# A four-layer image network on one NeuronCore: the parts of the last layer reordered into eighteen steps over six images, the adjusting in two halves

## The chip, the cores and the metric

The kernel runs on one NeuronCore of one Trainium2 chip. The metric is the device time of one execution in microseconds (us). The engines are named as in the profile: PE is TensorE (matrix multiplies, with PEld for its weight loads), DVE is VectorE, ACT is ScalarE, POOL is GpSimd, and SP is the engine whose queue starts the transfers. Each engine runs its own instructions in the order in which the program issues them; what one engine needs from another it waits for by semaphores.

## The reference, cut to what matters

The input is 32 images of 128 channels and 32 x 32 pixels, in float32. Four layers are applied, each as `x = x + layer(group_norm(x))`. The first is a 3 x 3 convolution, the second a state-space layer over the pixels, the third makes per-row and per-column maps with two more state-space scans, the fourth simulates a circuit of four qubits for each pixel. The change concerns the place where the third layer's maps are applied and the whole fourth layer:

```python
# end of layer 2: the maps of rows and columns are multiplied out, mixed, and scale the image
result_h = sigmoid(a_h) * x_y
result_w = sigmoid(a_w) * x_x
out1 = conv1x1(concatenate([result_h, result_w], axis=1), adjust_w)
return x * out1
...
# layer 3, on group_norm(x)
xq = xf @ pre_w.T + pre_b            # four angles for each pixel
z = simulate(xq, q_weights)          # sixteen amplitudes, squared and summed
out = z @ post_w.T + post_b
```

`group_norm` takes mean and variance over groups of four channels of one image.

## The kernel before

`images` and `attention` compute the first three layers up to the maps of rows and columns (`self.maps`), which stay in SBUF; the images themselves lie in DRAM as `self.x2`. The method `tail` then does the rest, image by image, with an image as a tile of 128 channels by 1024 pixels. It works through a software pipeline: a *turn* `j` issues each part once, for image `j - behind`, and `order` lists the parts with their distance `behind`. `manual_schedule` keeps the order of issue as written, so `order` is also the order of the instructions on each engine. A load of image `j` (`begin`) opens each turn.

What each part issues, and on which engine:

| part | instructions | lines |
|---|---|---|
| `begin` | SP: load of `xt`, 512 KB | L1407 |
| `outer` | POOL: products `rh`, `rw`; ACT: normalized image `xn` from `xt` | L1412, L1413, L1415 |
| `adjust` | PE: `adj` from `rh` and `rw`, two halves of 512 pixels | L1424, L1425 |
| `adjusted` | DVE: `xn` times `adj`, by halves; POOL: `xt` plus `xn` | L1430, L1431 |
| `sums` | DVE: statistics of the new `xt`, twice, and their union `gn_ag` | L1436, L1438 |
| `mean` | PE: means over the group of four channels | L1442 |
| `spread` | DVE: copy, difference, square (`gn_mv`, `gn_dv`) | L1446, L1447, L1448 |
| `variance` | PE: variance over the group | L1454 |
| `root` | DVE: add a constant; POOL: power -0.5 | L1457, L1458 |
| `normal` | DVE: `gn_mv`; ACT: x4, the normalized image | L1462, L1466 |
| `angles` | PE: `q` from x4, 16 rows for each half | L1471 |
| `rounded` | DVE: whole turns `kk` of the angles, two instructions | L1477, L1478 |
| `sines` | DVE: the rest `rr`; ACT: sine in place | L1482, L1485 |
| `states` | PE: `psi`, the amplitudes | L1490 |
| `squares` | ACT: `sq` | L1497 |
| `outputs` | PE: `outs`, two halves | L1503 |
| `end` | DVE: `xt` plus `outs`, two halves; SP: store of `xt`, 512 KB | L1510, L1513 |

The matrix products are in float32, so the profile shows two matmul instructions for each product of the program. Each product goes to a bank of PSUM of its own: two each for `adj` and `outs`, one each for `mean`, `variance`, `q` and `psi`, eight in all. `xt` has six buffers, all other tiles of an image three.

Of the kernel before, what the change touches and what calls it, by code (L numbers as in the profile page):

```python
# [12 lines left out]
F32 = mybir.dt.float32  # L13
BF16 = mybir.dt.bfloat16
AF = mybir.ActivationFunctionType
ALU = mybir.AluOpType
# [3 lines left out]
P = 128  # L20
S = 32
HW = S * S
# [532 lines left out]
class Steps:  # L555
# [11 lines left out]
    def run(self, ways, plan):  # L567

        k = self.k
        steps = [(w, h, n) for w in ways for h in range(2) for n in range(DS)]  # L570
        self.steps = steps
        for i in range(3):
            self.load(i)
        for i in range(3):
            self.decay(i)
        self.spread(0)
        self.input(0)
        for i in range(len(steps) + 2):
            self.evict()
            self.decay(i + 3)  # L580
            k.flush(False, vector=False)
            self.spread(i + 1)
            self.catch_up()
            self.scan(i)
            k.flush(False)
            self.input(i + 1)
            if self.has(i):
                plan.slot(i, self.load_of(i))
            self.scale(i + 4)
            self.weigh(i)  # L590
            self.add(i - 2)
            self.load(i + 3)
        self.evict()
        k.flush()
# [148 lines left out]
class Kernel:  # L743
# [630 lines left out]
    def tail(self):  # L1374
        tc, nc, d = self.tc, self.nc, self.d
        with ExitStack() as ctx:
            par = ctx.enter_context(tc.tile_pool(name="par3", bufs=1))
            img = ctx.enter_context(tc.tile_pool(name="img3", bufs=3))
            psl = ctx.enter_context(tc.tile_pool(name="psl3", bufs=3, space=PSUM))
            adj = par.tile([P, 2, P], F32, name="adj")  # L1380
# [14 lines left out]
            halves = [(32 * c, slice(c * 512, (c + 1) * 512)) for c in range(2)]  # L1395
# [7 lines left out]

            def begin(im, i):
                im.i = i
                im.xt = img.tile([P, HW], F32, tag="xt", name="xt", bufs=6)
                nc.sync.dma_start(im.xt, self.x2[i])  # L1407

            def outer(im):
# [7 lines left out]
                    scale=self.means[:, im.i, 2 * L + 1 : 2 * L + 2],  # L1417
                )

            def adjust(im):  # L1420
                im.adj = []
                for _, cs in halves:
                    ps = bank("adj", 2)
                    nc.tensor.matmul(ps, adj[:, 0], im.rh[:, cs], start=True, stop=False)  # L1424
                    nc.tensor.matmul(ps, adj[:, 1], im.rw[:, cs], start=False, stop=True)  # L1425
                    im.adj.append(ps)

            def adjusted(im):
                for ps, (_, cs) in zip(im.adj, halves):
                    nc.vector.tensor_tensor(im.xn[:, cs], im.xn[:, cs], ps, ALU.mult)  # L1430
                nc.gpsimd.tensor_tensor(im.xt, im.xt, im.xn, ALU.add)  # L1431

            def sums(im):
                st = tile_([P, 2, 6], "gn_st")
# [73 lines left out]
            def end(im):  # L1508
# [5 lines left out]


            order = [
                (sums, 3), (angles, 4), (mean, 3), (rounded, 4), (spread, 3), (variance, 3), (sines, 4),
                (root, 3), (adjust, 2), (states, 4), (adjusted, 2), (normal, 3), (squares, 4),
                (outputs, 4), (outer, 1), (end, 4),
            ]  # L1520
            with tc.manual_schedule():
                for j in range(self.n + 4):
                    if j < self.n:
                        begin(images[j], j)
                    for part, behind in order:
                        if 0 <= j - behind < self.n:
                            part(images[j - behind])
# [20 lines left out]
```

## Time and profile before

| quantity | value |
|---|---|
| median of 3 runs | 15073.83 us |
| lowest and highest of them | 15066.03 and 15084.82 us |
| profiled execution, its own time | 15093.06 us |
| its span | 15091.3 us |
| first instruction of `tail` on POOL (L1412) | 14599.22 us |
| time from there to the end of the span | 492.1 us |
| busy in the whole span: PE, DVE, ACT, POOL | 87%, 89%, 81%, 84% |
| busy in the 60 us from 14820 to 14880: PE, DVE, ACT, POOL | 41.03, 27.52, 13.97, 26.51 us |
| mean granted TensorE clock in these 60 us | 0.78 |

Lines of the profile read as follows. A group of instructions is given as line of the kernel, engine, operation, tile written, tiles read, shapes and count. On the timeline a row begins with the start and the duration in us; in brackets stand the idle time of the engine ahead of it and what ended it. In the list of waits, `A <- B: total, times, longest` says how long the first engine stood still ahead of that line until the second one's line was done. The three runs give the time that counts; the profile gives places and durations, from one execution that was 19.2 us longer than their median.

### The profile page before, as it was taken

What the parts mean: (1) busy time and instruction counts of PE and PEld (TensorE: products, weight loads), DVE (VectorE), ACT (ScalarE), POOL (GpSimd) and SP (SyncE); (2) the same over time, 40 slices, a digit from 0 to 9 for tenths busy, and PEclk for the clock granted to TensorE, in tenths of its full rate; (3) what the DMA queues carried; (4) which work ended last, traced back from release to release, by engine and by line L of the source; (5) the groups of instructions that cost most, each with busy time, mean ns of one, the idle gap of its engine ahead of it and who ended that gap; (6) DMA issues with size and microseconds to landing.
All of it is one profiled execution on the core that took longest, in us unless ns stands there. A gap on an engine that the chain in (4) does not pass through costs nothing. (4 is left out here: it accounts for less than half of the span.)

```text
span 15091.3 us, 197699 instructions
## 1 busy us (share of the span) xinstructions
PE 13174.8 (87%) x70318; PEld 8507.7 (56%) x70318; DVE 13401.1 (89%) x8776; ACT 12256.2 (81%) x21181; POOL 12747.8 (84%) x6529
## 2 busy tenths in 40 slices
PE   7888888888888888988888888888888888888876
PEld 4555555555555555555555555555555555555532
DVE  7999989999989999898999999999999999999774
ACT  6888888888888888888888888888888888888642
POOL 6888888888888888888888888888888888888764
PEclk8999999999999999999999999999999999999877
DMA  3444444444444444444444444444444444444431
GB/s 118 159 155 155 156 153 154 156 159 156 155 153 153 158 155 159 154 154 154 153 157 159 154 157 153 155 152 158 157 157 154 155 153 154 157 159 157 144 107 68
DMA packets 633895, 2277.61 MB, mean 151 GB/s; under 512 B 77481, under 2 KB 81145, under 8 KB 632777
## 3 DMA queue, kind: packets, MB, share of 16 engines
q1 hardware_dynamic: 630600, 2263.06, 43.8%
q8 instruction: 554, 9.08, 0.2%
q14 instruction: 437, 3.57, 0.1%
q10 hardware_dynamic: 2304, 1.90, 0.0%
HBM read 2221.35 MB, written 43.33 MB: 150 GB/s over the span
## 5 line engine op out<-in xcount | busy, mean ns | idle before, releaser
L686 POOL TENSOR_TENSOR hh<-hh,cc 128x1024 f32<-128x1024 f32 x4160 | 9771.8, 2366 | 1752.5 <-DVE hh L677 1086.5
L677 DVE TENSOR_TENSOR_SCAN hh<-da,bu 128x1024 f32<-128x1024 f32 x4160 | 9415.4, 2280 | 618.6 <-PE bu L647 234.9
L722 PEld LDWEIGHTS y<-cbig,hh 128*128 128x128 f32 x33280 | 4065.2, 150 | 1793.5 <-issue 1285.2
L722 PE MATMUL y<-cbig,hh 128*128 128x128 f32 x33280 | 4762.6, 290 | 181.8 <-POOL hh L686 181.4
L633 ACT ACTIVATE da<-dt,m_na 128x1024 f32<-128x1024 f32 x4096 | 4607.2, 1144 | 352.8 <-DVE hh L677 344.9
L669 DVE TENSOR_TENSOR bu<-du,bu 128x1024 f32<-128x1024 f32 x2752 | 3336.8, 1213 | 680.5 <-PE bu L653 679.6
L662 ACT ACTIVATE but<-dut,bt 128x128 f32<-128x128 f32 x11264 | 3433.6, 392 | 0.0
L653 PE MATMUL bu<-parts,sel 48*128 48x512 bf16 x5504 | 1761.5, 402 | 638.6 <-DVE hh L677 630.0
L280 PE MATMUL mm<-hpad,m_wc 128*128 128x512 f32 x4096 | 2063.6, 627 | 104.1 <-ACT relu L386 68.6
L647 PE MATMUL bu<-cbig,but 128*128 128x128 f32 x11264 | 1606.7, 290 | 378.1 <-DVE hh L677 331.6
L647 PEld LDWEIGHTS bu<-cbig,but 128*128 128x128 f32 x11264 | 1388.4, 151 | 445.2 <-issue 287.8
L280 PEld LDWEIGHTS mm<-hpad,m_wc 128*128 128x128 f32 x4096 | 710.1, 193 | 908.6 <-issue 753.5
L653 PEld LDWEIGHTS <-sel 48*128 48x128 bf16 x5504 | 322.6, 95 | 1149.9 <-DVE hh L677 687.2
L402 POOL TENSOR_TENSOR w<-w,du 128x1024 f32<-128x1024 f32 x260 | 613.8, 2361 | 38.3 <-ACT w L395 38.3
L299 PE MATMUL mm<-uc,m_xw 128*128 128x512 f32 x1024 | 602.9, 720 | 31.0 <-ACT sz L762 22.6
L701 PEld LDWEIGHTS y<-m_skip,uc 128*128 128x128 f32 x4096 | 554.4, 212 | 132.8 <-issue 79.8
L762 ACT ACT_TABLE_LOAD x483 | 619.7, 1283 | 8.5
L768 ACT ACT_TABLE_LOAD x483 | 619.7, 1283 | 8.5
L439 ACT COPY dut<-mm 128x512 f32<-128x512 f32 x512 | 294.9, 576 | 407.0 <-PE mm L434 406.9
L406 POOL TENSOR_TENSOR dt<-dt,w 128x1024 f32<-128x1024 f32 x260 | 615.3, 2366 | 0.2
L411 POOL TENSOR_TENSOR du<-dt,uc 128x1024 f32<-128x1024 f32 x260 | 614.3, 2363 | 0.2
L406 POOL TENSOR_TENSOR dt<-dt,relu 128x1024 f32<-128x1024 f32 x260 | 613.9, 2361 | 0.0
(219 smaller groups left out, 10394.3 us busy)
## 6 DMA issues: line engine op xcount, KB each, us to landing
cc<-rows SPq DMA_DIRECT2D x4160, 512.0 KB, 3.8
xt<-in_x SPq DMA_DIRECT2D x32, 512.0 KB, 5.9
x<-xt SPq DMA_DIRECT2D x32, 512.0 KB, 3.7
xt<-x SPq DMA_DIRECT2D x32, 512.0 KB, 4.0
out<-xt SPq DMA_DIRECT2D x32, 512.0 KB, 2.9
rows<-dbl SPq DMA_DIRECT2D x130, 64.0 KB, 4.3
stats<-st SPq DMA_DIRECT2D x32, 36.0 KB, 1.5
means<-stats SPq DMA_DIRECT2D x1, 1152.0 KB
```

Of the source, the lines that this page charges most:

```text
L280: nc.tensor.matmul(self.view(ps), m.wc[:, v, j, h * P : (h + 1) * P], self.taps(j, c), start=(j == 0), stop=(j == 3),)
L406: nc.gpsimd.tensor_tensor(self.dt[h], self.dt[h], t[name], op)
L633: k.nc.scalar.activation(t, w.dt[h], AF.Exp, scale=w.m.na[:, h, n : n + 1])
L647: k.nc.tensor.matmul(t[:, b * P : (b + 1) * P], but[:, b], k.ident, start=True, stop=True, is_transpose=True,)
L653: k.nc.tensor.matmul(t[:, cs], k.sel[:, n], w.parts[:, cs], start=True, stop=True)
L662: k.nc.scalar.activation(t[:, b], w.dut[h][:, b], AF.Copy, scale=w.bt[:, b, n : n + 1])
L669: k.nc.vector.tensor_tensor(t, w.du[h], t, ALU.mult)
L677: k.nc.vector.tensor_tensor_scan(way(t), way(self.da.pop(i)), way(self.bu.pop(i)), 0.0, ALU.mult, ALU.add)
L686: k.nc.gpsimd.tensor_tensor(t, t, self.cc.pop(i), ALU.mult)
L722: k.nc.tensor.matmul(self.y[g][: w.bl, b], t[:, at], k.ident, start=False, stop=(n == DS - 1 and b == w.per - 1), is_transpose=True,)
L762: self.nc.scalar.activation(*args, AF.Silu, **kw)
L768: self.nc.scalar.preload_act_table_set("natural_log_exp_and_others")
```

## The change

The order has eighteen steps instead of sixteen, since `adjust` and `adjusted` are each split into the two halves of 512 pixels. The distances are spread over six images instead of four: `adjust` and `adjusted` stay at 2 turns behind the load, the statistics (`sums` to `normal`) move from 3 to 4, the circuit from `angles` to `squares` from 4 to 5, and `outputs` and `end` from 4 to 6. The last turn is therefore `n + 5` instead of `n + 3`. `outer` moves from near the end of a turn to its front. `xt` has eight buffers instead of six.

```diff
             def begin(im, i):
                 im.i = i
-                im.xt = img.tile([P, HW], F32, tag="xt", name="xt", bufs=6)
+                im.xt = img.tile([P, HW], F32, tag="xt", name="xt", bufs=8)
                 nc.sync.dma_start(im.xt, self.x2[i])
...
-            def adjust(im):
-                im.adj = []
-                for _, cs in halves:
+            def adjust(c):
+                def run(im):
+                    _, cs = halves[c]
                     ps = bank("adj", 2)
                     nc.tensor.matmul(ps, adj[:, 0], im.rh[:, cs], start=True, stop=False)
                     nc.tensor.matmul(ps, adj[:, 1], im.rw[:, cs], start=False, stop=True)
-                    im.adj.append(ps)
-
-            def adjusted(im):
-                for ps, (_, cs) in zip(im.adj, halves):
-                    nc.vector.tensor_tensor(im.xn[:, cs], im.xn[:, cs], ps, ALU.mult)
-                nc.gpsimd.tensor_tensor(im.xt, im.xt, im.xn, ALU.add)
+                    im.adj = [*getattr(im, "adj", []), ps]
+                return run
+
+            def adjusted(c):
+                def run(im):
+                    xn = im.xn[:, halves[c][1]]
+                    nc.vector.tensor_tensor(xn, xn, im.adj[c], ALU.mult)
+                    if c:
+                        nc.gpsimd.tensor_tensor(im.xt, im.xt, im.xn, ALU.add)
+                return run
...
             order = [
-                (sums, 3), (angles, 4), (mean, 3), (rounded, 4), (spread, 3), (variance, 3), (sines, 4),
-                (root, 3), (adjust, 2), (states, 4), (adjusted, 2), (normal, 3), (squares, 4),
-                (outputs, 4), (outer, 1), (end, 4),
+                (outer, 1), (adjust(0), 2), (sums, 4), (angles, 5), (mean, 4), (rounded, 5),
+                (outputs, 6), (adjusted(0), 2), (spread, 4), (sines, 5), (adjust(1), 2),
+                (variance, 4), (end, 6), (root, 4), (adjusted(1), 2), (states, 5), (normal, 4),
+                (squares, 5),
             ]
             with tc.manual_schedule():
-                for j in range(self.n + 4):
+                for j in range(self.n + 6):
```

Line numbers in the text are those of the kernel before.

## The prediction

> **What bounds the kernel now.** I read the chain of work that ended last first: the largest lines in it, L1424, L1425 and L1503 among them, belong to the last layer (`tail`). Its first work, `rh`, starts at 14599.2 us and the span ends at 15091.3, so the change can touch 492 us, 3.3% of the span. Next the waits of that stretch, then one turn on the timeline. Waits (us in total, times, longest):
>
> ```profile
> ACT x L1466 <- DVE gn_mv L1462: 186.6, 32, 13.8
> ACT rr L1485 <- DVE rr L1482: 175.8, 32, 6.4
> DVE xn L1430 <- PE adj L1425: 147.3, 62, 3.6
> POOL xt L1431 <- DVE gn_mv L1462: 144.8, 26, 6.6
> DVE xt L1510 <- PE outs L1503: 108.1, 32, 5.6
> ```
>
> Every engine waits for another in every one of 32 turns: no engine is the bound, a ring through all of them is. In the windows view the stretch 14820 to 14880 has DVE busy 27.52 of 60 us, POOL 26.51, ACT 13.97, PE 41.03 at a mean clock of 0.78. One turn on DVE (start, us, engine, line):
>
> ```profile
> 14830.41 1.41 DVE L1510 SCALAR_TENSOR_TENSOR xt<-outs,vecs,xt 128x512 f32<-128x512 f32 x2 [3.03 <-PE outs L1503]
> 14831.74 1.27 DVE L1436 BATCH_NORM_STATS2 gn_st<-xt 128x6 f32<-128x512 f32 x2
> ...
> 14833.17 0.69 DVE L1477 TENSOR_SCALAR kk<-q,wb 64x512 f32<-64x512 f32 x1
> 14833.90 0.42 DVE L1478 TENSOR_SCALAR kk<-kk 64x512 f32<-64x512 f32 x1
> 14834.24 0.14 DVE L1446 COPY gn_mv<-mean 128x1 f32<-128x1 f32 x1
> 14834.42 0.16 DVE L1447 TENSOR_TENSOR gn_dv<-gn_ag,gn_mv 128x1 f32<-128x1 f32 x1
> 14834.61 0.22 DVE L1448 SCALAR_TENSOR_TENSOR gn_dv<-gn_dv,gn_ag 128x1 f32<-128x1 f32 x1
> 14834.75 0.74 DVE L1482 SCALAR_TENSOR_TENSOR rr<-q,wb,kk 64x512 f32<-64x512 f32 x1
> 14835.51 0.16 DVE L1457 TENSOR_SCALAR gn_dv<-variance 128x1 f32<-128x1 f32 x1
> 14838.89 0.69 DVE L1430 TENSOR_TENSOR xn<-xn,adj 128x512 f32<-128x512 f32 x1 [3.22 <-PE adj L1425]
> 14840.54 0.69 DVE L1430 TENSOR_TENSOR xn<-xn,adj 128x512 f32<-128x512 f32 x1 [0.96 <-PE adj L1425]
> 14841.14 0.15 DVE L1462 SCALAR_TENSOR_TENSOR gn_mv<-gn_mv 128x1 f32<-128x1 f32 x1
> ```
>
> The ring, start to start, from `normal` at 14827.23 to the next at 14841.14: to x4 on ACT 0.25, `squares` 1.15, `outputs` 0.62, `end` 1.16, `sums` 1.33, `variance` 3.15, `adjust` 0.45, the second `xn` 5.20, `normal` 0.60: 13.91. Turns are uneven because TensorE runs at two speeds: 4 adjusting matmuls take 1.81 us (14838.62 to the next part at 14840.43) or 3.56 (14804.87 to 14808.43). The mean turn, over 28 intervals of `rh`, is 14.76.
>
> [...]L1072, 0.26 us alone, has a median of 2.279 beside POOL's multiplies. [...]in the ramp L1447 once took 1.31 and L1478 1.79, ending with POOL's `rw`. Whether DVE gets in between two POOL instructions that follow at once is shown at 81 us, where every small L1344 has two SBUF inputs:
>
> ```profile
> 81.07 4.92 DVE L1344 SCALAR_TENSOR_TENSOR small<-small 64x8 f32<-64x8 f32 x3
> ...
> 81.33 2.34 POOL L402 TENSOR_TENSOR w<-w,du 128x1024 f32<-128x1024 f32 x1 [9.78 <-ACT w L395]
> ...
> 83.64 2.33 POOL L406 TENSOR_TENSOR dt<-dt,relu 128x1024 f32<-128x1024 f32 x1
> ...
> ```
>
> Three of them take 4.92 us instead of 0.73: two are held, one for each POOL instruction. So a held instruction gets in at the next boundary. [...]Here `adjust` begins slow after a nearly idle stretch (14831.4 to 14834.9) and its matmuls quicken about 3.3 us later[...].
>
> **The change, part by part.** No arithmetic is added or removed: per image DVE, ACT, POOL and PE issue the same instructions, and SP the same two DMAs. What moves is which image a part works on.
>
> *Cut links.* `sums` reads the `xt` of two turns ago, `outputs` the squares of the turn before, `angles` the x4 of the turn before, `adjust(0)` the products of the turn before. So of the old ring `squares`→`outputs`→`end`→`sums` and `variance`→`adjust`→`xn`→`normal` are gone. Left inside a turn is `angles`→`rounded`→...→`normal`→x4→next `angles`, because DVE runs in order. Start to start, from the turn above: `angles` to L1477 1.10 (1.05 and a signal); to L1478 0.73; to `adjusted(0)` 0.34; to `spread` 0.60; L1446 to L1447 0.18; to L1448 0.19; to L1482 0.14; to `end` 0.76; to `root` 1.33; `root` through POOL's power (0.31 + 0.55) to `normal` 0.89; to x4 0.25; x4 to `angles` 1.30. Sum **7.81**. `sums` (1.31) fits the 2.65 in which DVE waits for x4 and `angles`; if x4 came earlier it would lie on the path.
>
> *PE.* Full speed: two adjusting halves 3.62, `angles` 1.05, `outputs` 1.06, `states` 1.05, the two small sums 0.8: 7.6, all under 7.81. Half speed, from the slow rows: 7.12 + 1.92 + 1.88 + 1.92 + 1.17 = 14.0. Nothing in the old trace shows the clock under the new order; bounds 7.6 and 14.0. I take full speed: with turns under 10 us PE has work for over three quarters of the time and no gap over about 1.2.
>
> [...]POOL works 2.35 + 1.91 + 1.91 + 0.55 = 6.7 a turn; it used to do so while DVE mostly waited, now it runs beside DVE. Count from `normal` at 0: the `xt` addition starts at 0.17, `rh` at 2.48, `rw` at 4.35. `angles` starts at 1.55, L1478 wants 3.38: `rh` holds it to 4.38, **+1.0**. `rw` then starts late, to about 6.6; L1447 wants 5.50: **+1.1**. L1448 follows with POOL idle, free. Behind the held L1447 stand all later DVE instructions, and for it wait `variance`, `states` and the next `adjust(0)` on PE: they start later, but PE has 2 us to spare.
>
> A turn: 7.81 + 1.0 + 1.1 = **9.9**.
>
> *Ends.* 38 turns instead of 36. 27 have all parts (6 to 32). Turns 1 to 5 fill: I walk them to 35 us, bound by POOL (6.2 each) and the first load. After turn 32: one turn without products 7.8, two without adjusting 7.2 each, then 6.3 to the last squares, 2.1 for `outputs` at low clock, 1.4 for `end`, 3.7 as now from the last `end` to the span's end. Together 70.7.
>
> *Eight `xt` buffers.* Image i+8 takes the buffer that i leaves in turn i+6: never late. On SP each load stands behind one store, issued with `end`; it is needed over a turn later and lands in 4.0. Zero; with less than a turn of cover it would cost up to 4. In and out are 1 MB a turn, 106 GB/s where the page shows 150. At the start seven loads go out at once, not five; the first is not delayed by later ones.
>
> Sum: 14599.2 + 70.7 + 27 × 9.9 = 14937.2, against a span of 15091.3: **154 us less**. The profiled execution was 15093.06, 1.8 more than its span and 19.2 over the median; from 15073.83 that gives **14920**.
>
> **Rivals**, each by its turn in the same sum:
>
> 1. *The addition starts before `normal`.* `normal` can start 0.72 after the end of `root`, the addition about 0.75 after it. If POOL wins, `normal` is held 2.35, then L1478 0.44 and L1447 not: 10.6, giving 14939.
> 2. *No holds that matter*: 7.8, DVE and PE the bounds, 14863. Against it: L1072's times.
> 3. *More holds*: L1447 is let in at the end of `rh` and L1448 waits for `rw` too, +1.9: 11.8, giving 14971. The phase above speaks against it, not firmly.
> 4. *The clock stays halved*: PE bound at 14.0, giving 15030. Against it: busy for 3.3 us, it quickens.
> 5. *Slower.* `normal` loses to the addition and is held through POOL's whole run, addition, `rh` and `rw`: 6.15. PE then idles over 6 us a turn and starts slow: `angles` +0.9, and the slow `adjust(1)` puts `variance` 8.5 after `angles` where `root` wanted it at 6.2, +2.3. 7.8 + 6.15 + 3.2 = 17.2, giving 15117; it decides from a turn of 15.6. Against it: the boundaries at 81 us.
> 6. *The reading across turns fails*, another buffer or bank being reused within a turn: counting them, all are released in time (the eight PSUM banks by the same turn's DVE or ACT), and the turn would stay near 14.8. Chance with 4.
>
> **How the numbers follow.** Forecast 0.46, rival 1 0.20, 2 0.11, 3 0.11, 4 and 6 0.08, 5 0.04. The forecast is 14920; 14870 to 14990 holds forecast, 1, 3 and part of 2. Under 0.2% (30 us, about what a measurement can tell from no change) is a turn of 14.5 to 16.7: 0.02 of case 4 and 6. Faster 0.94, same 0.02, slower 0.04.
>
> **What would show it.** `rh` every 9.9 us; L1478 and L1447 with medians over a microsecond; L1424 near 0.43 a matmul; ACT's wait for L1462 small; the same busy sums per image. A turn near 8 without held instructions, or near 14 with slow matmuls, would make the prediction wrong.

## The result, and the profile after

| | before | after |
|---|---|---|
| median of 4 runs, us | 15076.30 | 14926.87 |
| lowest and highest, us | 15066.03, 15084.82 | 14924.63, 14935.45 |
| ratio of the times, 95% interval | | 0.9901 [0.9889, 0.9914] |
| profiled execution: own time, span, us | 15093.06, 15091.3 | 14935.45, 14933.7 |
| first `rh` of `tail` to the end of the span, us | 492.1 | 345.3 |

The changed kernel is 149 us faster, about 1%. Of the 157.6 us between the two spans, 146.8 lie in `tail`. The other 10.8 are an earlier start of `tail`, behind code that is the same in both kernels; such starts differed by up to 26 us among the profiled executions of this study. So experiments are compared below by their **tail time**, first `rh` to the end of the span, beside their medians.

The changed kernel's line numbers are higher by up to 4: `rh` L1412, `rw` L1413, `adjust` L1424 and L1425, `xn` times `adj` L1432, the addition L1434, statistics L1440 and L1442, `mean` L1446, `spread` L1450 to L1452, `variance` L1458, `root` L1461 and L1462, `normal` L1466 and L1470, `angles` L1475, `rounded` L1481 and L1482, `sines` L1486 and L1489, `states` L1494, `outputs` L1507, `end` L1514. Below, K2 is the second instruction of `rounded` (L1482), and TT the difference in `spread` (L1451).

The waits of `tail` after the change (us in total, times, longest):

```profile
ACT rr L1489 <- DVE rr L1486: 153.0, 32, 5.9
POOL gn_mv L1462 <- DVE gn_dv L1461: 111.1, 31, 7.7
DVE kk L1481 <- PE q L1475: 75.8, 32, 4.4
ACT x L1470 <- DVE gn_mv L1466: 61.7, 32, 11.4
```

The waits that made the old ring are small or gone: ACT's for `normal` fell from 186.6 to 61.7 us, DVE's for `adj` from 147.3 to 3.1 and for `outs` from 108.1 to 4.1, and POOL's for `gn_mv` before the addition is not among the largest. DVE's one regular wait is for `angles`, as the shortened ring says. Here is a whole turn on DVE (start, us, engine, line), from one `normal` to the next, 9.35 us:

```profile
14770.38 0.16 DVE L1466 SCALAR_TENSOR_TENSOR gn_mv<-gn_mv 128x1 f32<-128x1 f32 x1
...
14773.04 0.74 DVE L1481 TENSOR_SCALAR kk<-q,wb 64x512 f32<-64x512 f32 x1 [1.06 <-PE q L1475]
14773.82 1.11 DVE L1482 TENSOR_SCALAR kk<-kk 64x512 f32<-64x512 f32 x1
14774.85 0.67 DVE L1432 TENSOR_TENSOR xn<-xn,adj 128x512 f32<-128x512 f32 x1
14775.44 0.14 DVE L1450 COPY gn_mv<-mean 128x1 f32<-128x1 f32 x1
14775.62 1.09 DVE L1451 TENSOR_TENSOR gn_dv<-gn_ag,gn_mv 128x1 f32<-128x1 f32 x1
14776.74 0.22 DVE L1452 SCALAR_TENSOR_TENSOR gn_dv<-gn_dv,gn_ag 128x1 f32<-128x1 f32 x1
...
14778.92 0.67 DVE L1432 TENSOR_TENSOR xn<-xn,adj 128x512 f32<-128x512 f32 x1
14779.73 0.16 DVE L1466 SCALAR_TENSOR_TENSOR gn_mv<-gn_mv 128x1 f32<-128x1 f32 x1
```

POOL in the same turn:

```profile
14770.38 2.40 POOL L1434 TENSOR_TENSOR xt<-xt,xn 128x1024 f32<-128x1024 f32 x1
14772.73 1.92 POOL L1412 TENSOR_TENSOR rh<-maps 128x1024 f32<-128x1024 f32 x1
14774.60 2.10 POOL L1413 TENSOR_TENSOR rw<-maps 128x1024 f32<-128x1024 f32 x1
```

K2 takes 1.11 us (0.42 undisturbed) and ends in the 0.3 us after `rh`; TT takes 1.09 (0.16 undisturbed) and ends with `rw`. These are the two held instructions. `normal` and the addition begin in the same instant, 14770.38, and `normal` is not held.

Not every turn is like this one. The 27 full turns, between 14620.69 and 14891.84, average 10.04 us and come in three kinds: 10 short ones of 9.35, 13 middle ones of 10.28, 4 long ones of 11.03. The matmuls of the middle turn that starts at 14760.10:

```profile
14760.27 2.08 PE L1424 MATMUL adj<-rh,adj 128*128 128x512 f32 x2
14762.14 1.25 PE L1425 MATMUL adj<-rw,adj 128*128 128x512 f32 x2
14763.31 1.05 PE L1475 MATMUL q<-x,wt 128*32 128x512 f32 x4
```

In the short turn the same `adj` pairs take 1.13 and 1.02 us; here the first takes 2.08. `adjust(0)` stands ahead of `angles` on PE, so `angles` starts 3.21 us after `normal` instead of 1.56 (14771.94). What DVE does then:

```profile
14764.42 0.74 DVE L1481 TENSOR_SCALAR kk<-q,wb 64x512 f32<-64x512 f32 x1 [2.71 <-PE q L1475]
14765.19 1.31 DVE L1482 TENSOR_SCALAR kk<-kk 64x512 f32<-64x512 f32 x1
14767.20 0.16 DVE L1451 TENSOR_TENSOR gn_dv<-gn_ag,gn_mv 128x1 f32<-128x1 f32 x1
```

DVE's wait grows from 1.06 to 2.71; K2 is held by `rw` and TT, now later than all of POOL's run, is free: +1.65 for the wait, +0.20 for K2, -0.93 for TT, which is 10.27. In a long turn L1481 starts 3.3 us later than in a short one, and neither K2 nor TT is held: 9.35 + 3.3 - 1.62 = 11.03. The durations of K2 and TT over all turns (minimum, median, maximum, ns):

```profile
L1482 DVE TENSOR_SCALAR kk<-kk x32: 418/1109/1347, 14616.8 to 14921.9; 64x512 f32<-64x512 f32 x32
...
L1451 DVE TENSOR_TENSOR gn_dv<-gn_ag,gn_mv x32: 159/160/1089, 14605.9 to 14914.3; 128x1 f32<-128x1 f32 x32
```

K2 is held in most turns, TT in the short ones alone.

What makes the three kinds shows in the granted clock, read in steps of 3.41 us. The windows view gives the stretch, its length, busy us and count of PE, PEld, DVE, ACT and POOL, then the mean clock, the DMA share and GB/s:

```profile
14776.23:14779.64 3.41, 1.67 (x8) 0.71 (x8) 3.32 (x7) 0.63 (x1) 0.96 (x2) 1.00 0.00 0
14779.64:14783.06 3.42, 3.42 (x6) 0.89 (x7) 1.56 (x4) 2.85 (x3) 3.39 (x3) 0.50 0.87 307
...
14786.47:14789.88 3.41, 2.38 (x9) 0.67 (x8) 3.33 (x9) 0.63 (x1) 0.46 (x1) 1.00 0.00 0
14789.88:14793.30 3.42, 3.42 (x6) 0.89 (x7) 1.57 (x4) 2.85 (x3) 3.39 (x3) 0.50 0.87 307
```

In the full turns the clock is 1.00 or 0.50 for whole multiples of 3.41 us. There are 17 slow stretches: 13 of 3.41 us, one for each middle turn, and 4 of 6.83, one for each long turn. Half clock for 3.41 us costs 1.71 us of work (an estimate from these two figures); DVE's wait for `angles` grows by 1.65 in 11 of the 13 middle turns and by 3.3 in the long ones. Each slow stretch follows a step in which PE was busy for 70% of the time or less, here 1.67 and 2.38 us. Five other steps of 70 to 71% kept the clock, and so did all from 78% on.

### The profile page after: what moved, and what is told of

It reads as the page before. It is cut to its first block, busy times and chain, and to the rows that moved or that the text cites. A ratio compares the mean times of both kernels' runs of the same rounds, so it can differ in the third digit from the quotient of the medians.

```text
span 14933.7 us, 197665 instructions
## 1 busy us (share of the span) xinstructions
PE 13134.9 (88%) x70318; PEld 8476.3 (57%) x70318; DVE 13425.4 (90%) x8776; ACT 12255.0 (82%) x21181; POOL 12760.0 (85%) x6529
```

## The experiments

The theory: a ring of 7.8 us is left; POOL's instructions hold K2 (by 0.69 us) and TT (by 0.93); and TensorE's clock, which falls from 1.00 to 0.50 because those holds leave PE idle, makes the longer turns. The rivals were that the distances alone bring the gain, that the halves don't matter, that the slow matmuls only fill time in which all wait anyway, and that with the holds gone something else takes their place. All runs, with the time of `tail` and of one turn from their profiles; each ratio is to the kernel before as it was timed again in the same series (its medians lay between 15076.30 and 15087.32 us), so that ratios compare better than medians:

| kernel | median, us | ratio to before [95%] | tail, us | turn, us |
|---|---|---|---|---|
| after | 14926.87 | 0.9901 [0.9889, 0.9914] | 345.3 | 9.35, 10.28, 11.03 |
| `e1_five_images` | 14948.45 | 0.9905 [0.9890, 0.9921] | 352.1 | mostly 10.27 |
| `e2_second_half_twice` | 14921.88 | 0.9888 [0.9875, 0.9902] | 328.0 | 9.35 |
| `e3_old_order` | 15059.02 | 0.9982 [0.9974, 0.9990] | 467.1 | 13.65 |
| `e4_no_holds` | 14858.35 | 0.9848 [0.9835, 0.9862] | 263.0 | 7.27 |
| `e5_seven_buffers` | 14939.35 | 0.9907 [0.9890, 0.9923] | 345.0 | as after |
| `e6_together` | 14995.79 | 0.9941 [0.9926, 0.9956] | 399.0 | 11.1 and 12.8 |
| `e7_one_hold_less` | 14901.97 | 0.9879 [0.9865, 0.9894] | 313.4 | 8.85, 9.09 |
| `e8_stats_only` | 14874.63 | 0.9864 [0.9849, 0.9879] | 290.3 | 8.20 |
| `e9_before_no_holds` | 15053.28 | 0.9978 [0.9971, 0.9985] | 455.5 | 13.28, 14.6 to 14.7 |

**Are the slow matmuls a cause?** The products of the second adjusting half are issued twice, the second time over the first: more work on PE, nothing less anywhere.

```diff
-                    nc.tensor.matmul(ps, adj[:, 0], im.rh[:, cs], start=True, stop=False)
-                    nc.tensor.matmul(ps, adj[:, 1], im.rw[:, cs], start=False, stop=True)
+                    for _ in range(1 + c):
+                        nc.tensor.matmul(ps, adj[:, 0], im.rh[:, cs], start=True, stop=False)
+                        nc.tensor.matmul(ps, adj[:, 1], im.rw[:, cs], start=False, stop=True)
```

> The changed kernel with the products of adjust(1) issued twice, the second time over the first in the same bank: 1.8 us more work for PE in each turn, put where PE waits for variance and the sines. Theory (the turns of 10.3 and 11.0 us come from the TensorE clock, halved by PE's gaps after adjust(1), so that the next adjust(0) takes 3.5 instead of 1.8 and angles queues behind it): with the gap filled the clock stays full, adjust(0) takes 1.8 in every turn, every turn is the short kind of 9.35: 27 x 0.7 = 19 us less than the changed kernel, about 14908. Rival (PE is near its bound, added work adds time): turns of 10.5 to 12, 14940 to 14980.

The windows view from 14700 to 14760, first after, then this kernel:

```profile
14700.00:14760.00 60.00, 53.62 (x144) 16.57 (x142) 42.21 (x88) 20.12 (x24) 39.51 (x24) 0.84 0.29 99
```

```profile
14700.00:14760.00 60.00, 58.30 (x179) 21.83 (x180) 51.90 (x97) 21.01 (x25) 44.49 (x26) 1.00 0.31 106
```

The clock goes from 0.84 to 1.00, all 27 turns take 9.35 us (9.31 to 9.38), and both holds are there in nearly every turn (K2, one line lower here, and TT):

```profile
L1483 DVE TENSOR_SCALAR kk<-kk x32: 418/1101/1115, 14626.5 to 14913.2; 64x512 f32<-64x512 f32 x32
...
L1452 DVE TENSOR_TENSOR gn_dv<-gn_ag,gn_mv x32: 158/1086/1090, 14615.9 to 14905.5; 128x1 f32<-128x1 f32 x32
```

Some 1.7 us more of matmuls in a turn (the second issue runs from 14702.73 to 14704.45 in one of them) make `tail` 17.3 us shorter. The intervals of the two ratios overlap, so it is the profiles that decide here: the clock is a cause, and it is worth what the mean turn says, 27 x (10.04 - 9.35) = 19 us.

**Do the holds make the turn, and what is behind them?** K2 goes, and TT gets an operand in PSUM. The turns are rounded in one instruction instead of two: `kk` keeps the large constant, and `rr` takes it off, with its sign turned in the sine. In the statistics the copy goes, and the difference is written to PSUM beside the mean, so that no instruction has two inputs in SBUF:

```diff
-                nc.vector.tensor_scalar(im.kk, im.kk, MAGIC, None, ALU.subtract)
...
-                    im.rr, im.q[:64], wb, im.kk, ALU.add, ALU.subtract
+                    im.rr, im.kk, MAGIC, im.q[:64], ALU.subtract, ALU.subtract
...
-                nc.scalar.activation(im.rr, im.rr, AF.Sin, scale=TWO_PI)
+                nc.scalar.activation(im.rr, im.rr, AF.Sin, scale=-TWO_PI, bias=turned)
...
-                nc.vector.tensor_copy(im.mv[:, 0:1], im.ps[:, 0:1])
-                nc.vector.tensor_tensor(im.dv, im.ag[:, 0:1], im.mv[:, 0:1], ALU.subtract)
+                im.pm = im.ps
+                off = im.pm[:, 1:2]
+                nc.vector.tensor_tensor(off, im.ag[:, 0:1], im.pm[:, 0:1], ALU.subtract)
...
-                    im.dv, im.dv, im.dv, im.ag[:, 1:2], ALU.mult, ALU.add
+                    im.dv, off, off, im.ag[:, 1:2], ALU.mult, ALU.add
...
-                    mv[:, 0:1], mv[:, 0:1], -1.0, mv[:, 1:2], ALU.mult, ALU.mult
+                    mv[:, 0:1], im.pm[:, 0:1], -1.0, mv[:, 1:2], ALU.mult, ALU.mult
```

(`turned` is the offset `wb` times 2 pi, computed once.)

> The changed kernel[...]: the second kk instruction is gone (rr is taken from the biased kk and q in PSUM, the sine gets the offset as its bias), the difference from the mean is written to and read from PSUM, and the copy of the mean is gone. Theory[...]: holds vanish, with the two instructions' own 0.5 the DVE chain is 7.3, PE at 7.6 or more becomes the bound; turns of 8.0 to 8.5, some 1.5 to 2 x 27 = 40 to 54 less than the changed kernel: 14873 to 14887. Rival (the long durations beside POOL are only waiting for something else that ends then): only the 0.5 of the two instructions is gained, 14913.

The turn is 7.27 us, shorter than expected. PE in one turn:

```profile
14769.64 1.13 PE L1426 MATMUL adj<-rh,adj 128*128 128x512 f32 x2
14770.60 1.02 PE L1427 MATMUL adj<-rw,adj 128*128 128x512 f32 x2
14771.55 1.05 PE L1478 MATMUL q<-x,wt 128*32 128x512 f32 x4
...
14772.85 1.13 PE L1509 MATMUL outs<-sq,wz 32*128 32x512 f32 x4
14773.91 1.12 PE L1426 MATMUL adj<-rh,adj 128*128 128x512 f32 x2
14774.87 1.02 PE L1427 MATMUL adj<-rw,adj 128*128 128x512 f32 x2
14775.73 0.28 PE L1461 MATMUL variance<-gn_dv,cbig 128*128 128x1 f32 x2
14775.93 1.05 PE L1496 MATMUL psi<-rr,ut 32*32 32x512 f32 x4
```

Each row starts before the one ahead of it has ended, none shows a wait, and the windows view has PE busy for 59.95 of 60 us at clock 1.00. So the next bound is PE, at full clock. The expected 8.0 to 8.5 was too high: I had counted 7.6 or more for PE's work and left room for gaps, but back to back a turn's matmuls take 7.27. This is the fastest version of the study: 1.5% under the kernel before, 0.5% under the changed one. It issues DVE work differently, so it is a further change and not part of the one predicted.

**One hold at a time.** Only the edit of `rounded` and `sines`:

> The changed kernel without the second kk instruction (rr is taken from the biased kk and q in PSUM, the sine gets the offset as its bias); the small statistics instructions keep their two SBUF inputs. Theory[...]: the hold moves to the next instructions with two SBUF inputs: the difference (gn_dv from gn_ag and gn_mv) now comes up near the end of rh, and the square behind it is held through all of rw, 1.6 to 1.8 us in the usual turn; turns near 8.9, 14890 to 14905. Rival (no hold moves: whatever is not the second kk keeps its duration or is free): turns of 8.0 to 8.4, 14873 to 14883.

DVE in one turn of 8.85 us:

```profile
14751.92 0.67 DVE L1434 TENSOR_TENSOR xn<-xn,adj 128x512 f32<-128x512 f32 x1
...
14752.69 0.16 DVE L1453 TENSOR_TENSOR gn_dv<-gn_ag,gn_mv 128x1 f32<-128x1 f32 x1
14752.89 1.76 DVE L1454 SCALAR_TENSOR_TENSOR gn_dv<-gn_dv,gn_ag 128x1 f32<-128x1 f32 x1
```

POOL runs `rh` here from 14750.85 and `rw` from 14752.72 for 1.91 us. With K2's 1.1 us gone, TT arrives just at the boundary between the two and slips in (0.16); the square behind it, free in the changed kernel, takes 1.76 instead of 0.22 and ends with `rw`. The hold moved to the next instruction with two inputs in SBUF, as the theory said: TT, 0.03 us ahead of `rw`, is free, and the square, 0.17 us behind its start, waits it out.

Only the edit of the statistics, with K2 left as it was:

> The changed kernel with the second kk instruction as it is, but the difference from the mean written to and read from PSUM, so that the small statistics instructions have one SBUF input, and without the copy of the mean. Theory[...]: the second kk alone is held, 0.7 to 0.9 us; with the gap between adjust(1) and variance gone the clock stays full and no turn is of the long kinds; turns of 8.2 to 8.4, 14876 to 14890. Rival (the hold comes back on another instruction, as the sum of POOL's and DVE's work has to be paid somewhere): turns of 9.0 or more, above 14897.

The windows view, then POOL and DVE in one turn:

```profile
14700.00:14760.00 60.00, 54.00 (x178) 19.29 (x177) 50.81 (x104) 24.67 (x29) 50.39 (x30) 1.00 0.35 125
```

```profile
14717.81 2.08 POOL L1413 TENSOR_TENSOR rw<-maps 128x1024 f32<-128x1024 f32 x1
...
14718.65 0.15 DVE L1452 TENSOR_TENSOR mean<-gn_ag,mean 128x1 f32<-128x1 f32 x1
```

All turns but the first ones take 8.20 us: TT's hold is gone (9.35 - 8.20 = 1.15; 0.93 of hold and the copy), K2's remains at 1.1, and the clock is 1.00. The difference, with one input in PSUM, isn't held beside POOL: it starts while `rw` runs and takes 0.15 us, where TT, with both in SBUF, took 1.09 in the changed kernel; the square, with one input left in SBUF, takes 0.22.

**Distances without the sequence.** The new distances, but the parts in the old order, both halves together:

```diff
-                (outer, 1), (adjust(0), 2), (sums, 4), (angles, 5), (mean, 4), (rounded, 5),
-                (outputs, 6), (adjusted(0), 2), (spread, 4), (sines, 5), (adjust(1), 2),
-                (variance, 4), (end, 6), (root, 4), (adjusted(1), 2), (states, 5), (normal, 4),
-                (squares, 5),
+                (sums, 4), (angles, 5), (mean, 4), (rounded, 5), (spread, 4), (variance, 4), (sines, 5),
+                (root, 4), (adjust(0), 2), (adjust(1), 2), (states, 5), (adjusted(0), 2),
+                (adjusted(1), 2), (normal, 4), (squares, 5), (outputs, 6), (outer, 1), (end, 6),
```

> The distances of the change (2, 4, 5, 6 turns) and eight buffers, but the parts in the sequence of the kernel before, both halves of the adjusting together, outer near the end. Theory (most of the gain is from the distances, which cut the ring; the sequence adds the rest, since here adjust stands between variance and normal): turns of about 11.5 (variance at 6.7 behind the holds, adjusting to 10.3, normal at 11), some 12.5 at low clock: 14965 to 14990, ratio 0.993 to 0.995. Rival (the eighteen steps and the halves are what counts): turns near the old 14.8, above 15040.

My theory fell here: a turn is 13.65 us, not 11.5. DVE in one turn:

```profile
14825.81 1.41 DVE L1514 SCALAR_TENSOR_TENSOR xt<-outs,vecs,xt 128x512 f32<-128x512 f32 x2 [1.27 <-PE outs L1507]
...
14829.30 1.69 DVE L1482 TENSOR_SCALAR kk<-kk 64x512 f32<-64x512 f32 x1
...
14835.76 0.69 DVE L1432 TENSOR_TENSOR xn<-xn,adj 128x512 f32<-128x512 f32 x1 [3.42 <-PE adj L1425]
14837.41 0.69 DVE L1432 TENSOR_TENSOR xn<-xn,adj 128x512 f32<-128x512 f32 x1 [0.96 <-PE adj L1425]
14838.01 0.15 DVE L1466 SCALAR_TENSOR_TENSOR gn_mv<-gn_mv 128x1 f32<-128x1 f32 x1
```

No data link asks for it, but in the queues `adjust` still stands behind `variance` on PE and `normal` behind `adjusted` on DVE. So the adjusting matmuls, half of them slow and 5.3 us in all from 14832.00, are still in the ring through the order of issue, and DVE waits 3.42 and 0.96 for them. K2 is held (1.69) besides. The distances alone give 28 of the 149 us. The new sequence with the old distances was not run.

**Halves apart or together.** The second half right behind the first at the front of the turn:

```diff
-                (outer, 1), (adjust(0), 2), (sums, 4), (angles, 5), (mean, 4), (rounded, 5),
-                (outputs, 6), (adjusted(0), 2), (spread, 4), (sines, 5), (adjust(1), 2),
+                (outer, 1), (adjust(0), 2), (adjust(1), 2), (sums, 4), (angles, 5), (mean, 4), (rounded, 5),
+                (outputs, 6), (adjusted(0), 2), (spread, 4), (sines, 5),
```

> The changed order with adjust(1) moved to directly behind adjust(0), at the front of the turn; all distances and the places of adjusted(0) and adjusted(1) as in the change. Theory (the halves matter since one half of 1.8 us fits under x4 on ACT, 1.55 after normal, and the other under DVE's work; both together stand in front of angles): angles starts 3.3 instead of 1.55 after normal at full clock, 5 where the clock is low; turns of 10.5 to 11.5, 14940 to 14970. Rival (only the distances between the parts count, not where the halves stand on PE): turns as in the changed kernel, 14927.

PE in one turn whose `normal` is at 14795.72:

```profile
14796.24 2.08 PE L1424 MATMUL adj<-rh,adj 128*128 128x512 f32 x2
14798.10 1.91 PE L1425 MATMUL adj<-rw,adj 128*128 128x512 f32 x2
14799.81 1.74 PE L1424 MATMUL adj<-rh,adj 128*128 128x512 f32 x2
14801.38 1.02 PE L1425 MATMUL adj<-rw,adj 128*128 128x512 f32 x2
14802.34 1.05 PE L1475 MATMUL q<-x,wt 128*32 128x512 f32 x4
```

Both halves now stand ahead of `angles`, most of it at half clock, and `angles` starts 6.6 us after `normal`. K2 takes 0.42 in this turn: so late, it is beyond POOL's run. The turns, 11.1 and 12.8, average about 12. The direction was right, the size too small: `angles` starts 4.9 us after `normal` in the shorter turns, near the 5 that I had put for a low clock, but 6.6 in the others. Placing the second half where PE would be idle is worth 54 us of `tail`.

**Five images instead of six.** Statistics, circuit, `outputs` and `end` each one turn nearer to the load, so 37 turns:

```diff
-                (outer, 1), (adjust(0), 2), (sums, 4), (angles, 5), (mean, 4), (rounded, 5),
...
+                (outer, 1), (adjust(0), 2), (sums, 3), (angles, 4), (mean, 3), (rounded, 4),
...
-                for j in range(self.n + 6):
+                for j in range(self.n + 5):
```

> The changed order, but each distance from the statistics on one turn shorter, so that sums reads the image that POOL's addition finished in the turn just before, not two turns before; 37 turns. Theory (what reads preceding work must read it early enough to fit where DVE waits anyway): sums waits for the addition to about 2.5 us after normal, ends at 4.0 instead of 2.7, the first kk starts 1.3 later in the turns whose q comes early, and the second kk then meets rw instead of rh. Turns of about 10.6 where the changed kernel has a mean of 10.0, one short turn less: about 14938, ratio to before 0.991, and a wait of DVE's gn_st for POOL's xt of 1 us or more in each turn. Rival (one turn of distance is enough, the sums lie in DVE's idle time whatever they read): turns of 10.0, one of 7 less, 14920, no such wait.

`sums` now waits for the addition of the preceding turn:

```profile
DVE gn_st L1440 <- POOL xt L1434: 72.6, 32, 2.5
```

That is 2.3 us a turn, as expected, but it mostly takes the place of DVE's wait for `angles`: nearly all turns are of the middle kind, 10.27, so only the short turns are lost. With one turn less to run, `tail` is 6.8 us longer than after. The ratio, 0.9905, can't be told from the changed kernel's. The sixth image brings little by itself.

**Buffers.** `bufs=7` for `xt` instead of 8:

> The changed kernel with seven xt buffers instead of eight (six can't be had: a load would wait for a store behind it on SP's own queue). Theory (the buffers cost and give nothing): each load now waits for the landing of the store just ahead of it, 3 us, still a turn before xn needs it; turns of 9.35 to 11.0 with a mean of 10.0, 14915 to 14940. Rival (the eighth buffer covers the load): ACT's xn waits for the load in each turn by 1 to 4 us, 14960 to 15030.

`tail` takes 345.0 us against 345.3, with the same kinds of full turns; the whole times can't be told apart. In the queue of SP 25 loads do wait for a store now, 60.7 us in all, but `xn` on ACT waits for loads no longer than with eight (6.8 us against 6.7). The eighth buffer does nothing for the time.

**The holds in the old order.** The kernel before, with the two edits of the kernel without holds:

> The kernel before the change, with the edits of the two hold experiments together: no second kk instruction, difference from the mean through PSUM, no copy of the mean. Theory (the holds are a cost that the change brought in, since before it POOL ran while DVE waited): nothing is held here, so only the two instructions' own 0.5 us a turn go from the ring, 0.5 x 33 = 17 us: 15050 to 15065, ratio 0.9975 to 0.9993. Rival (the edits are worth the same in any order): the 70 us that they gave on the changed order, ratio near 0.995.

It gains 33 us, between the two expectations. In the kernel before, K2 (L1478) takes 0.42 in every turn from 14642.5 to 15055.8: it is not held. Turns now take 13.28 us in about three of four and 14.6 to 14.7 in the others, where the kernel before has 13.91, 14.98 and 15.48 in turn. So the short turns are 0.63 us shorter; that the longer ones are also rarer is only seen in their times, not tested by itself. The two edits take 37 us off the old kernel's `tail` and 82 off the changed one's: over half of what they bring there comes only with the new order.

## Why the prediction was right, step by step

The forecast, 14920 us by two holds and a turn of 9.9, met 14926.87. Part of the agreement is luck: the holds came out smaller than forecast, so that a short turn is 9.35 and not 9.9, and the clock that I had left out puts 0.69 back on the mean turn.

- **The cut ring, 7.81: right.** A short turn less its two holds, 9.35 - 0.69 - 0.93, is 7.73; and the largest waits moved as said. The kernel with the old sequence shows that the distances alone don't cut it: the order of issue has to change with them.
- **K2's hold by `rh`, +1.0: right in place, 0.69 in size.** Counted from `normal`, K2 began at 3.44 (I had 3.38) and `rh` ended at 4.27, not 4.35 or more, since the addition started at 0.00 and not at 0.17; and once released K2 needed 0.28, not the 0.42 that I had left it. In middle turns `rw` holds it, 0.9.
- **TT's hold by `rw`, +1.1: right in mechanism and size (0.93), wrong in how often.** I took it for every turn, with a median over a microsecond; it comes in 10 of 27 turns, with a median of 0.16. With the clock filled it comes in all of them. That nothing else on DVE would be held in the turn was my estimate; `xn` (L1432) and the copy did run beside the same `rw` in 0.67 and 0.14 us.
- **"I take full speed": the step that failed.** The argument was that PE has "no gap over about 1.2". The gaps are indeed about that short: in the short turn shown PE ends `adjust(1)` at 14776.27 and until `states` at 14778.39 runs only `variance`, 0.38 us, between gaps of 0.74 and 0.99; in a middle turn only the gap of 0.99 is left. But both lost the clock, 1.00 in the step and 0.50 in the next, with PE busy for 1.67 and 2.38 us of a step of 3.41. The old trace has such a step too, half busy with a single gap of 1.69 us:

```profile
14811.03:14814.44 3.41, 1.72 (x8) 0.31 (x8) 0.76 (x2) 1.94 (x3) 1.98 (x1) 1.00 0.02 5
14814.44:14817.86 3.42, 3.42 (x8) 0.40 (x8) 1.61 (x3) 0.91 (x1) 3.42 (x3) 0.50 0.00 0
```

I had let `variance` and `states` start later because "PE has 2 us to spare"; that spare time is what cost the clock: with the second issue in it the clock over 60 us is 1.00 instead of 0.84. It reaches the ring because `adjust(0)` stands ahead of `angles`: +0.93 in 13 turns and +1.68 in 4, 19 us in all. That gaps this short keep the clock was my estimate; no trace of before showed it. The grid of the steps of 3.41 us does not follow the turns of 9.35 and 10.28, and a step with PE busy for 1.67 us, about half of it, was enough for half clock in the next. That middle turns come in rows fits the grid, since 10.28 is nearly three steps (10.24); I have not tested it. What decides among steps of about 70% stays open.
- **The sum.** 27 turns measure 271.2 us, predicted 267.3; fill and drain 74.1, predicted 70.7. Together `tail` is 7.3 us longer than the predicted 338.0. Outside it two more terms nearly cancel: `tail` began 10.8 us earlier than in the trace before, and the profiled execution was 8.6 us over the median where I had taken 19.2.
- **Costs of nothing.** Eight buffers and the transfers: borne out, by the run with seven and by the absence of any wait for a load among the largest. The first load landed 4.03 us after its issue with seven at once, against 4.18 with the five of before.
- **Rival 1**, the addition ahead of `normal`: it is a tie, and `normal` came through in each of the full turns, where the two start within 0.01 us or `normal` is ahead; once in the ramp, at 14610.41, the addition had begun 0.06 us earlier, and `normal` took 2.29. **Rival 2**, no holds, 7.8: excluded by the K2 rows; with both holds removed, and two instructions with them, the turn is even a little less. **Rival 3**, more holds: the square was free, until K2 was removed. **Rival 4**: the clock fell in part (0.84 in the window above), not to half, and no turn came near 14. **Rival 5**: where `normal` lost, it was held for one POOL instruction, 2.29, and not for three. **Rival 6**: no wait for a buffer was seen.

## What to carry to other kernels

Where engines run in order, as here (with the old sequence DVE waited 3.42 and 0.96 us in a turn for matmuls that no data link put there), look at the ring through the queues and not only at the data: the same distances in another sequence gave a fifth of the gain. Once engines overlap that used to take turns, look which small instructions are held by the neighbour's long ones (here 1.11 us instead of 0.42 and 1.09 instead of 0.16), and put one of their operands in PSUM or do without them; here the first was worth 55 us of `tail`, both together 82. And before taking TensorE's full clock for granted, count its busy share over the steps in which the trace shows the clock change (3.41 us here, with half clock after 1.67 us of work in one), not gap by gap; keep the matmuls that start slow from standing ahead of the one that the ring waits for.

## What the runs showed that I had not expected

- More matmuls made `tail` shorter: doubling one pair raised the mean clock from 0.84 to 1.00 and took 17.3 us off.
- The busy share of PE over 60 us does not tell the clock: 53.62 of 60 us went with 0.84, 54.00 with 1.00. The first figure holds slow matmuls, which look busy nearly twice as long (1.92 us for a pair instead of 1.02).
- When `normal` on DVE and the addition on POOL began in the same instant, as at 14770.38, DVE's was not held, in any of the full turns. A lag of 0.06 us was enough to be held for 2.29: at 14610.41 after the change, and at 14868.51 with seven buffers. With the mean read from PSUM the same lag cost nothing (`e8_stats_only` at 14606.52: 0.16 us).
